# A graph layer with four gated experts on one core: a join of partitions at step 90 of the experts' loop, intermediate rows in one tensor per group, a sixth buffer in the last stage

## The chip, the cores and the metric

The kernel runs on one NeuronCore of a Trainium2 chip. The metric is the device time of one execution in microseconds (us). Before the change it is 4193.42 us, the median of 3 runs (4192.93 to 4193.94).

## What is computed

x holds 12500 nodes of 256 float32 features. Two layers are added to it, one after the other. (The helper functions of the second are written here as one line each.)

```python
x = x + gnn(layernorm(x), src, dst, edge_weight, W, b)      # 200000 edges
x = x + ffn(layernorm(x), ...)                              # 131072 edges + a loop at each node

def gnn(z, src, dst, w, W, b):
    agg = segment_sum(z[src] * w[:, None], dst)
    return agg @ W.T + b

def ffn(x, ...):                       # HEADS = 4, NUM_EXPERTS = 4, TOP_K = 2
    h = (x @ W_gat).reshape(M, 4, 4)
    e = leaky_relu((h * att_src).sum(-1)[src] + (h * att_dst).sum(-1)[dst], 0.2)
    alpha = softmax of e over the edges of one dst, for each head
    agg = segment_sum(h[src] * alpha[:, :, None], dst).reshape(M, 16) + b_gat
    scores = layernorm(agg, ln_gamma, ln_beta).reshape(M, 4, 4).mean(1)
    w = softmax(top 2 of scores)
    for ei in range(4):
        out += gate(w, ei) * (gelu(x @ W1[ei] + b1[ei]) @ W2[ei] + b2[ei])
```

So each node needs two things at the end: four rows of 256 from the four experts, which depend on the node alone, and four gates, which depend on a softmax over the edges that end at it. The edges of this second graph start and end at nodes below 8192; the other nodes have the loop only.

## The kernel before, in words

Nodes are padded to 98 tiles of 128 (`NT`) and worked on in 25 groups of 4 tiles (`GT`, `NG`; the last group has 2 tiles).

**Stage 1**, up to about 2230 us: layer norm; POOL gathers the rows of the 200000 edges (L550) and PE adds them up with one-hot products (L564). Beside it the 131072 edges of the second graph are sorted by their end.

**Stage 2, the nodes**: `node_out` makes `x2 = x + agg W^T + b` and stores it, two groups at a time, to the DRAM tensor `X2` (`x2_rows`). Then come the norm (stored turned, `y_t`), and the small features of the attention (`gat_nodes`). The profile leaves digits at the end of a word out of names: `x2_rows` shows as `x_rows`, `po5` and `po4` as `po`, `o5` as `o`.

**Stage 3, the experts**, from 2495 to 3916 us. A loop over `step` goes through 100 pairs of (group, expert), and step 100 ends the last. Step s issues on PE, half by half, `up` of pair s (products with W1, L942, then Gelu on ACT, L948, into `hh`) and `down` of pair s - 1 (products with W2, L966, into one of two PSUM buffers `po5`; then DVE adds b2, L970, into `fo`). After two experts of a group SP stores `fo` to `FO` (`expert_rows`, L974). The order of PE is written by hand in this loop (`tc.manual_schedule`): what is issued inside it on PE keeps its place. The other engines get their order from the scheduler of the framework, and each runs its own in order.

Under the experts runs the attention. The sorted edges lie on 128 partitions, 1024 columns each (`L2`), edge after edge. POOL gathers 11 columns (`PER_TURN`) of `G` per step (L809), held back so that it is no more than `LEAD` = 4 steps ahead. As soon as all columns of a `block` (128 columns; the last two are 896 to 991 and 992 to 1023) are there, DVE and ACT do a running maximum, exponentials and running sums on it (L880 to L902), in some eight parts by `yield`, one part per step, and SP stores the finished columns to `gat_run` in DRAM. The condition ahead of a block is `(step - 2) * PER_TURN >= blocks[0][1]`, so that it comes two steps behind its columns. What is left after step 100 is issued behind the loop.

**The join.** A node's edges may be split between two partitions. So the values at the end of each partition are carried on to the next: column 1024 of `G` is turned (`carried`: two PE transposes, a scan on DVE, one transpose back), with an Exp on ACT between maxima and sums. That is six PE transposes in all. Then POOL gathers one row per partition from `gat_run` (the row at which the first node of the partition ends, `row<-gat_run,fix_i`), it is corrected (`fixed`), and POOL scatters it back. All that stands behind the loop.

**Stage 4, the gates and the mix.** SP loads three small rows (L1062) and `nodes` (`gat_nodes` again, 1.2 MB, L1068). `gates(t0, n)` works on four stretches of tiles: 0 to 11, 12 to 35, 36 to 79, 80 to 97. For each tile POOL gathers one row of `gat_run` per node (`R`, L1082: the row at which the node's edges end, and for a node without edges one row at the end of the table); then follow some 50 DVE instructions with Exp, Sqrt and Exp on ACT (L1098 to L1145). `R` has two buffers, so that a third stretch waits for the first. `mixed(g)` loads `fo_in` (2 MB, L1151) and the rows of x2 (`o5`, 0.5 MB, L1154) on SP, in the pool `mix` of five buffers; per tile ACT makes a diagonal matrix (L1158), PE adds x2 and the expert of index 3 (L1160, L1161), DVE adds the other three (L1163); ACT stores to `out` (L1166). `issue_after` puts the gates of a stretch behind the last `mixed` of the stretch before.

The pools of stage 4 open after those of stage 3 are closed, and lie on the same memory.

Of the kernel before, what the change touches and what calls it, by code (L numbers as in the profile page):

```python
# [23 lines left out]
F32 = mybir.dt.float32  # L24
# [4 lines left out]
AF = mybir.ActivationFunctionType  # L29
ALU = mybir.AluOpType  # L30
AX = mybir.AxisListType
PSUM = bass.MemoryType.PSUM
# [20 lines left out]
GT = 4  # L53
# [7 lines left out]
def gnn_gat_moe(ctx, tc, x, src, dst, edge_weight, W, b, W_gat, att_src, att_dst, b_gat, ln_gamma,  # L61
# [3 lines left out]
    Z = nc.dram_tensor("z_rows", (NPAD, D), F32).ap()  # L65
    WT = nc.dram_tensor("w_turned", (D, D), F32).ap()
    STARTS = nc.dram_tensor("gat_starts", (E2 + NPAD, SEG), F32).ap()
    X2 = nc.dram_tensor("x2_rows", (NPAD, D), F32).ap()
    YT = nc.dram_tensor("y_t", (P, NT, 2, P), F32).ap()
    FO = nc.dram_tensor("expert_rows", (NPAD, C, D), F32).ap()  # L70
    NODE = nc.dram_tensor("gat_nodes", (NPAD, ROW), F32).ap()
    RUN2 = nc.dram_tensor("gat_run", (E2 + P, ROW), F32).ap()

# [12 lines left out]
    def node_rows(table, t0, n):  # L86
        return table[t0 * P:(t0 + n) * P, :].rearrange("(t p) d -> p t d", p=P)
# [569 lines left out]
    with ExitStack() as s2:  # L657
# [57 lines left out]
        def node_out(g):  # L715
            f, (t0, n, _) = flow[g], rows_of(g)
            if g % 2 == 0:
                f["x2_two"] = gp.tile([P, 2 * GT, D], F32, name="x2_two", bufs=2)
            x2_two = flow[g - g % 2]["x2_two"]
            x2 = f["x2"] = x2_two[:, g % 2 * GT:(g % 2 + 1) * GT]  # L720
            for i, m in pairs(n):
                po = ps.tile([P, 2, D], F32, name="po")
                for a in range(m):
                    for k in range(2):
                        nc.tensor.matmul(po[:, a, :], f["agt"][:, i + a, k, :], w_t[:, k, :],
                                         start=(k == 0), stop=(k == 1))
                nc.vector.tensor_add(x2[:, i:i + m, :], f["x"][:, i:i + m, :], po[:, :m, :])
            if g % 2 or g == NG - 1:
                m = g % 2 * GT + n
                nc.sync.dma_start(node_rows(X2, t0 + n - m, m), x2_two[:, :m, :])  # L730
            f["y"] = gp.tile([P, GT, D], F32, name="y")
            f["stats"] = statistics(small, x2, n)

# [50 lines left out]
    with ExitStack() as s3:  # L784
# [11 lines left out]
        low = big.tile([P, 1], F32, name="low")  # L796
        fix_i = big.tile([P, 1], I32, name="fix_i")
        spot = big.tile([P, 8], F32, name="spot")
        pre = tc.alloc_tile_pool(name="pre", bufs=1)
        far = pre.tile([P, L2], F32, name="far")  # L800
        nc.gpsimd.iota(far, pattern=[[1, L2]], base=0, channel_multiplier=0,
# [72 lines left out]
        def block(a, z):  # L874
# [21 lines left out]
            for ch in range(NS):  # L896
                if ch % 4 == 0:
# [4 lines left out]
            nc.sync.dma_start(RUN2[:E2, :].rearrange("(p l) c -> p l c", l=L2)[:, a:z, :],  # L902
                              G[:, a + 1:z + 1, :])


        blocks = [(a, min(a + 128, L2 - 32)) for a in range(0, L2 - 32, 128)] + [(L2 - 32, L2)]
        under_way = None
        with ExitStack() as s5:
# [46 lines left out]
            def down(item, half):  # L955

                g, e = item["at"]
                t0, n, _ = rows_of(g)
                if half == 0 and e % 2 == 0:
                    fos[g] = io.tile([P, GT, 2, D], F32, name="fo")  # L960
                if 2 * half < n:
                    po = pe.tile([P, 2, D], F32, name="po5", bufs=2)
                    for a in range(2):
                        i = 2 * half + a
                        for f in range(NF):
                            m = nc.tensor.matmul(po[:, a, :], item["hh"][:, f, i * P:(i + 1) * P],  # L966
                                                 w_2[:, e, f, :], start=(f == 0), stop=(f == NF - 1))
                            if half == a == f == 0:
                                after_all(m, item["there"])
                    item["last"] = nc.vector.tensor_add(  # L970
                        fos[g][:, 2 * half:2 * half + 2, e % 2, :], po,
                        b_2[:, e, None, :].to_broadcast([P, 2, D]))
                if half and e % 2:
                    nc.sync.dma_start(FO[t0 * P:(t0 + n) * P, e - 1:e + 1, :].rearrange(  # L974
                        "(t p) e d -> p t e d", p=P), fos[g][:, :n])

            yts, fos, freed = {}, {}, [[], []]
# [2 lines left out]
            with tc.manual_schedule(engines={mybir.EngineType.PE}):  # L980
                old = None
                for step in range(NG * C + 1):
                    new = dict(at=divmod(step, C)) if step < NG * C else None
                    for half in range(2):
                        if new:
                            up(new, half)
                        if old:
                            down(old, half)
                    if old:
                        turned.append(old["last"])  # L990
                        gathers(len(turned) - 1 + LEAD)
                    old = new

                    if under_way is None and blocks and (step - 2) * PER_TURN >= blocks[0][1]:
                        under_way = block(*blocks.pop(0))
                    if under_way and next(under_way, under_way) is under_way:
                        under_way = None
        for _ in under_way or ():
            pass
        for a, z in blocks:  # L1000
            for _ in block(a, z):
                pass


        tail = s3.enter_context(tc.tile_pool(name="tail", bufs=1))
        end = G[:, L2, :]
        m0 = tail.tile([P, H], F32, name="m0")
        carried(tail, low.to_broadcast([P, H]), end[:, NS:], H, ALU.add, ALU.max, LOW, m0)

        def joined(m_in, s_in, m_own, name):  # L1010

            m = tail.tile([P, H], F32, name="m_" + name)
            nc.vector.tensor_max(m, m_in, m_own)
            f = tail.tile([P, 2, H], F32, name="f_" + name)
            nc.vector.tensor_sub(f[:, 0, :], m0, m)
            nc.vector.tensor_sub(f[:, 1, :], m_own, m)
            nc.scalar.activation(f, f, AF.Exp)
            return m, f

        def by_head(v, f):  # L1020

            s = tail.tile([P, NS], F32, name="by_head", bufs=2)
            nc.vector.tensor_mul(s[:, :HC].rearrange("p (h c) -> p h c", c=C),
                                 v[:, :HC].rearrange("p (h c) -> p h c", c=C),
                                 f[:, :, None].to_broadcast([P, H, C]))
            nc.vector.tensor_mul(s[:, HC:], v[:, HC:NS], f)
            return s

        m_in = tail.tile([P, H], F32, name="m_in")
        nc.vector.tensor_scalar(m_in, m0, low, None, ALU.add)  # L1030
        _, f = joined(m_in, None, end[:, NS:], "end")
        nc.vector.tensor_scalar(f[:, 0, :], f[:, 0, :], through, None, ALU.mult)
        v = by_head(end, f[:, 1, :])
        fs = tail.tile([P, NS], F32, name="fs")
        nc.vector.tensor_copy(fs[:, :HC].rearrange("p (h c) -> p h c", c=C),
                              f[:, 0, :, None].to_broadcast([P, H, C]))
        nc.vector.tensor_copy(fs[:, HC:], f[:, 0, :])
        s0 = tail.tile([P, NS], F32, name="s0")
        carried(tail, fs, v, NS, ALU.mult, ALU.add, 0.0, s0)

        row = tail.tile([P, ROW], F32, name="row")
        nc.gpsimd.indirect_dma_start(out=row, out_offset=None, in_=RUN2,
                                     in_offset=IND(ap=fix_i, axis=0))
        fixed = tail.tile([P, ROW], F32, name="fixed")
        m, f = joined(m0, None, row[:, NS:], "row")
        s_in, s_own = by_head(s0, f[:, 0, :]), by_head(row, f[:, 1, :])
        nc.vector.tensor_add(fixed[:, :NS], s_in, s_own)
        nc.vector.tensor_copy(fixed[:, NS:], m)
        nc.gpsimd.indirect_dma_start(out=RUN2, out_offset=IND(ap=fix_i, axis=0), in_=fixed,
                                     in_offset=None)  # L1050


    with ExitStack() as s4:
        one = s4.enter_context(tc.tile_pool(name="one", bufs=1))
        some = s4.enter_context(tc.tile_pool(name="some", bufs=2))
        mix = s4.enter_context(tc.tile_pool(name="mix", bufs=5))
        turn = s4.enter_context(tc.tile_pool(name="turn", bufs=4))
        ps = s4.enter_context(tc.tile_pool(name="ps4", bufs=6, space=PSUM))

        def along_nodes(ap, name):  # L1060
            t = one.tile([P, HC], F32, name=name)
# [85 lines left out]
        def mixed(g):  # L1147

            t0, n, rows = rows_of(g)
            fo = mix.tile([P, GT, C, D], F32, name="fo_in")  # L1150
            nc.sync.dma_start(fo[:, :n], FO[t0 * P:(t0 + n) * P].rearrange(  # L1151
                "(t p) e d -> p t e d", p=P))
            xo = mix.tile([P, GT, D], F32, name="o5")
            nc.sync.dma_start(xo[:, :n, :], node_rows(X2, t0, n))  # L1154
            for i in range(n):
                g4 = gate[:, t0 + i, :]
                diag = turn.tile([P, P], F32, name="diag")
# [46 lines left out]
```

## Time and profile before

| | us |
|---|---|
| median of 3 runs | 4193.42 |
| the profiled execution | 4198.22 |
| its span | 4196.4 |
| PE busy | 3552.0 (85%) |
| POOL busy | 2906.0 (69%) |
| DVE busy | 2393.0 (57%) |
| ACT busy | 1421.4 (34%) |
| 3500 to 3916 (experts): PE busy; DMA share; GB/s | 399.99 of 416; 0.22; 59 |
| 3916 to 4196 (join and last stage): PE busy; DVE busy; DMA share; GB/s | 125.19 of 280; 193.81; 0.91; 286 |

The profile is of one execution. Its page has a row per engine with the busy share of 40 equal slices of the span, in tenths, and a row with the GB/s that the DMA engines moved. A window view gives for any stretch its length, the busy time and number of instructions of PE, PE's weight loads, DVE, ACT and POOL, the clock granted to PE (1.00 is full), the share of 16 DMA engines that were busy, and GB/s. A timeline gives start, duration, engine, line and tiles of each instruction; in brackets stands the idle time ahead and what ended it. The chain of waits goes back from the last instruction to what released each step. The largest steps of it that lie near the end are loads and stores, and the gathers of `R`:

```profile
3942.41 5.74 DMA R<-gat_run,end
...
4024.91 49.50 DMA fo_in<-expert_rows
4074.42 10.90 DMA o<-x_rows
4098.46 10.38 DMA out<-o
```

### The profile page before, as it was taken

Reading aid. Unit: us, or ns where it says so; the run is one execution under the profiler, and the core shown is the slowest. Engines: PE = TensorE matmul, PEld = TensorE weight load, DVE = VectorE, ACT = ScalarE, POOL = GpSimd, SP = SyncE. Lnnn points to the kernel's source line nnn. Section 1 sums busy time; section 2 is a strip of 40 time slices with the busy share of each in tenths; the row PEclk is TensorE's granted clock in tenths of the full one; section 3 lists DMA queues with packets and bytes.
Section 4 is the critical chain, followed back from the end, with each engine's and each line's share of the span. In section 5 each row is a group of like instructions: output and inputs, shape, how many; then the busy total and the mean of one; then the engine's idle time right before and its main releaser. Section 6 shows DMA issues by size and latency. Waiting matters only on the chain. (4 is left out here: it accounts for less than half of the span.)

```text
span 4196.4 us, 54596 instructions
## 1 busy us (share of the span) xinstructions
PE 3552.0 (85%) x18969; PEld 2610.1 (62%) x18970; DVE 2393.0 (57%) x5474; ACT 1421.4 (34%) x3289; POOL 2906.0 (69%) x2855
## 2 busy tenths in 40 slices
PE   1466899999999999999998959999989999899545
PEld 0365676767766667767677836666656666566424
DVE  7566777878787878787778950221211202212477
ACT  4322445445545444545452211221212212212122
POOL 2577777777777777777776777777777777773440
PEclk6688999999999999999999969999999999999767
DMA  7433333333333333333335652222222222221698
GB/s 234 135 93 93 102 102 100 100 100 101 100 101 100 99 101 101 100 101 100 99 102 157 191 145 60 67 72 55 64 50 75 75 55 64 65 60 62 206 226 346
DMA packets 265845, 457.42 MB, mean 109 GB/s; under 512 B 67943, under 2 KB 168705, under 8 KB 264289
## 3 DMA queue, kind: packets, MB, share of 16 engines
q0 software_dynamic: 114128, 219.11, 21.4%
q1 hardware_dynamic: 111663, 207.52, 14.0%
q10 hardware_dynamic: 39778, 27.28, 2.1%
q8 instruction: 153, 2.51, 0.2%
q14 instruction: 123, 1.01, 0.1%
HBM read 334.05 MB, written 119.66 MB: 108 GB/s over the span
## 5 line engine op out<-in xcount | busy, mean ns | idle before, releaser
L550 POOL DMA_INDIRECT gt<-z_rows,src x1563 | 1605.2, 1027 | 592.2 <-issue 410.2
L809 POOL DMA_INDIRECT G<-gat_nodes,order x1024 | 1026.5, 1002 | 339.3 <-issue 289.0
L564 PE MATMUL win<-gt,oh_w 128*128 128x256 f32 x3126 | 770.1, 398 | 200.4 <-DMA gt<-z_rows,src 149.3
L564 PEld LDWEIGHTS win<-gt,oh_w 128*128 128x128 f32 x3126 | 598.0, 198 | 317.0 <-issue 188.4
L966 PE MATMUL po<-w,hh 128*128 128x256 f32 x3136 | 724.3, 385 | 51.4 <-ACT hh L948 38.3
L966 PEld LDWEIGHTS po<-w,hh 128*128 128x128 f32 x3136 | 605.5, 193 | 220.8 <-issue 87.1
L970 DVE TENSOR_TENSOR fo<-po,b 128x512 f32<-128x512 f32 x196 | 135.3, 690 | 1016.6 <-PE po L966 1016.6
L942 PE MATMUL ph<-yt,w 128*128 128x512 f32 (+1 forms) x1600 | 707.8, 586 | 2.8 <-DMA w<-in_L_ffn_W 2.8
L556 ACT ACTIVATE oh_w<-hit_w,w 128x128 f32<-128x128 bf16 x1563 | 500.9, 390 | 448.2 <-PE win L564 226.6
L490 DVE TENSOR_SCALAR st<-along,place_l,code 128x1024 bf16<-128x1024 f16 x1024 | 550.3, 578 | 162.3 <-PE perm L498 161.7
L948 ACT ACTIVATE hh<-ph,b 128x512 f32<-128x512 f32 (+1 forms) x400 | 249.3, 676 | 1001.6 <-PE ph L942 1001.5
L498 PE MATMUL perm<-st,to_p 128*128 128x512 bf16 x2048 | 524.1, 378 | 0.0
L942 PEld LDWEIGHTS ph<-yt,w 128*128 128x128 f32 x1600 | 305.0, 191 | 292.5 <-issue 277.9
L454 PE MATMUL look<-next,oht 98*128 98x128 f32 x2044 | 393.8, 300 | 0.0
L454 PEld LDWEIGHTS look<-next,oht 98*128 98x128 f32 x2044 | 309.6, 192 | 37.5
L462 ACT ACTIVATE next<-place 98x256 f32<-98x256 f32 x511 | 196.1, 384 | 345.1 <-PE place L459 344.3
L469 DVE TENSOR_TENSOR sel<-look,oh_lo 128x512 f32<-128x512 f32 x256 | 174.9, 683 | 186.4 <-PE look L454 185.2
L498 PEld LDWEIGHTS <-to_p 128*128 128x128 bf16 x2048 | 178.5, 97 | 122.3 <-DVE st L490 0.4
L571 DVE SCALAR_TENSOR_TENSOR acc_x<-win,in,acc_x 128x256 f32 x522 | 246.9, 473 | 8.7 <-PE win L564 8.6
L450 PE MATMUL look<-oh_lo,same_hi 128*128 128x128 bf16 x1024 | 228.1, 223 | 1.2 <-ACT next L462 1.0
L442 ACT ACTIVATE same_hi<-bank 128x512 bf16<-128x512 f32 x256 | 152.8, 597 | 215.2 <-PE bank L440 215.1
L340 DVE TENSOR_TENSOR oh_hi<-twice,hi 128x784 bf16<-128x784 bf16 x256 | 143.4, 560 | 100.6 <-PE place L364 100.5
(278 smaller groups left out, 3641.8 us busy)
## 6 DMA issues: line engine op xcount, KB each, us to landing
expert_rows<-fo SPq DMA_DIRECT2D x48, 1024.0 KB, 4.2
fo_in<-expert_rows SPq DMA_DIRECT2D x24, 2048.0 KB, 16.4
gt<-z_rows,src POOLq DMA_INDIRECT x1563
G<-gat_nodes,order POOLq DMA_INDIRECT x1024
xt<-in_x SPq DMA_DIRECT2D x24, 512.0 KB, 4.8
z_rows<-xt ACTq DMA_DIRECT2D x24, 512.0 KB, 4.6
x_two<-in_x SPq DMA_DIRECT2D x12, 1024.0 KB, 6.4
x_rows<-x_two SPq DMA_DIRECT2D x12, 1024.0 KB, 10.6
```

Of the source, the lines that this page charges most:

```text
L450: first = nc.tensor.matmul(look[:, i % GT + k, :], b["m"][:, i + k, :], one(b["ol"], i + k), start=True, stop=False)
L454: nc.tensor.matmul(look[:, i % GT + k, :], b["oht"][:, i + k, :], nxt[:, k, :], start=False, stop=True)
L490: last = nc.vector.tensor_scalar(st[:, k, :], along, b["l"][:, i + k:i + k + 1], code2[:, c:c + 1], ALU.is_equal, ALU.mult)
L498: first = nc.tensor.matmul(perm[:, h, :], one(b["p"], i + k), st[:, k, h * 512:(h + 1) * 512], start=(c == 0), stop=(c == NC2 - 1), skip_g ...
L550: there = [nc.gpsimd.indirect_dma_start(out=rows[j], out_offset=None, in_=Z, in_offset=IND(ap=idx[:, c:c + 1], axis=0)) for j, c in enumer ...
L556: there += [nc.scalar.activation(hots[j], one(hit, j), AF.Copy, scale=w[:, c:c + 1]) for j, c in enumerate(chunks)]
L564: i = nc.tensor.matmul(win, h, r, start=(j == 0), stop=(j == len(rows) - 1))
L571: return nc.vector.scalar_tensor_tensor(to, win, m, to, ALU.mult, ALU.add)
L809: i = nc.gpsimd.indirect_dma_start(out=G[:, t + 1, :], out_offset=None, in_=NODE, in_offset=IND(ap=order[:, t:t + 1], axis=0))
L942: i = nc.tensor.matmul(ph[:, :n], w_1[:, e, k, f * P:(f + 1) * P], yts[g][:, :n, k, :], start=(k == 0), stop=(k == 1))
L948: i = nc.scalar.activation(item["hh"][:, f, :n * P], ph[:, :n].rearrange("p t m -> p (t m)"), AF.Gelu, bias=b_1[:, e * NF + f:e * NF + f + 1])
L966: m = nc.tensor.matmul(po[:, a, :], item["hh"][:, f, i * P:(i + 1) * P], w_2[:, e, f, :], start=(f == 0), stop=(f == NF - 1))
```

## The change

Six edits, in stages 2 to 4.

1. `X2` becomes one DRAM tensor per two groups, and `FO` one per group, instead of one each; stores and loads use the part that they need.
2. A block no longer comes two steps behind its columns. The block of columns 896 to 991 counts as there at column 990, which is step 90. When only the last two blocks are left (and none is under way), all parts that are left are issued in one step, in place of one part per step.
3. The join becomes a function, `join()`, and is called in the loop where the last block ends. Its code is that of before, but for a copy: column 1024 is copied into a tile `end` first, so that `join` reads that. The pool `tail` opens at the start of stage 3.
4. Stores of `fo` of the last three groups (22 to 24) are issued by ScalarE's queue in place of SP's.
5. The pools of stage 4 get `reuse_waits="tile"`: a tile waits for the tiles that lay on its own memory, rather than for all of a pool's.
6. `mix` has six buffers in place of five.

```diff
-    X2 = nc.dram_tensor("x2_rows", (NPAD, D), F32).ap()
+    X2 = [nc.dram_tensor(f"x2_rows{g}", (2 * GT * P, D), F32).ap() for g in range((NG + 1) // 2)]
-    FO = nc.dram_tensor("expert_rows", (NPAD, C, D), F32).ap()
+    FO = [nc.dram_tensor(f"expert_rows{g}", (GT * P, C, D), F32).ap() for g in range(NG)]
...
+        def join():
+            end = tail.tile([P, ROW], F32, name="end")
+            nc.vector.tensor_copy(end, G[:, L2, :])
...
-                    nc.sync.dma_start(FO[t0 * P:(t0 + n) * P, e - 1:e + 1, :].rearrange(
+                    queue = nc.sync if g < NG - 3 else nc.scalar
+                    queue.dma_start(FO[g][:n * P, e - 1:e + 1, :].rearrange(
...
-                    if under_way is None and blocks and (step - 2) * PER_TURN >= blocks[0][1]:
-                        under_way = block(*blocks.pop(0))
-                    if under_way and next(under_way, under_way) is under_way:
-                        under_way = None
-        for _ in under_way or ():
-            pass
-        for a, z in blocks:
-            for _ in block(a, z):
-                pass
...
+                    for _ in range(1 if len(blocks) > 2 or under_way and len(blocks) == 2 else 20):
+                        if under_way is None and blocks and step * PER_TURN >= min(
+                                blocks[0][1], (L2 - 32) // PER_TURN * PER_TURN):
+                            under_way = block(*blocks.pop(0))
+                        if under_way and next(under_way, under_way) is under_way:
+                            under_way = None
+                            if not blocks:
+                                join()
+                assert not blocks and under_way is None
...
-        mix = s4.enter_context(tc.tile_pool(name="mix", bufs=5))
+        mix = s4.enter_context(tc.tile_pool(name="mix", bufs=6, reuse_waits="tile"))
...
-            nc.sync.dma_start(fo[:, :n], FO[t0 * P:(t0 + n) * P].rearrange(
-                "(t p) e d -> p t e d", p=P))
+            nc.sync.dma_start(fo[:, :n], FO[g][:n * P].rearrange("(t p) e d -> p t e d", p=P))
-            nc.sync.dma_start(xo[:, :n, :], node_rows(X2, t0, n))
+            nc.sync.dma_start(xo[:, :n, :], node_rows(X2[g // 2], g % 2 * GT, n))
```

More of the change, by code (lines that the diff above doesn't have):

```diff
@@ L729, in node_out @@
                 m = g % 2 * GT + n
-                nc.sync.dma_start(node_rows(X2, t0 + n - m, m), x2_two[:, :m, :])
+                nc.sync.dma_start(node_rows(X2[g // 2], 0, m), x2_two[:, :m, :])
             f["y"] = gp.tile([P, GT, D], F32, name="y")
@@ L798, in gnn_gat_moe @@
         spot = big.tile([P, 8], F32, name="spot")
+        tail = s3.enter_context(tc.tile_pool(name="tail", bufs=1))
         pre = tc.alloc_tile_pool(name="pre", bufs=1)
@@ L903, in block, with joined, by_head @@
                               G[:, a + 1:z + 1, :])
+        def join():
+            end = tail.tile([P, ROW], F32, name="end")
+            nc.vector.tensor_copy(end, G[:, L2, :])
+            m0 = tail.tile([P, H], F32, name="m0")
+            carried(tail, low.to_broadcast([P, H]), end[:, NS:], H, ALU.add, ALU.max, LOW, m0)
+            def joined(m_in, s_in, m_own, name):
+                m = tail.tile([P, H], F32, name="m_" + name)
+                nc.vector.tensor_max(m, m_in, m_own)
+                f = tail.tile([P, 2, H], F32, name="f_" + name)
+                nc.vector.tensor_sub(f[:, 0, :], m0, m)
+                nc.vector.tensor_sub(f[:, 1, :], m_own, m)
+                nc.scalar.activation(f, f, AF.Exp)
+                return m, f
+            def by_head(v, f):
+                s = tail.tile([P, NS], F32, name="by_head", bufs=2)
+                nc.vector.tensor_mul(s[:, :HC].rearrange("p (h c) -> p h c", c=C),
+                                     v[:, :HC].rearrange("p (h c) -> p h c", c=C),
+                                     f[:, :, None].to_broadcast([P, H, C]))
+                nc.vector.tensor_mul(s[:, HC:], v[:, HC:NS], f)
+                return s
+            m_in = tail.tile([P, H], F32, name="m_in")
+            nc.vector.tensor_scalar(m_in, m0, low, None, ALU.add)
+            _, f = joined(m_in, None, end[:, NS:], "end")
+            nc.vector.tensor_scalar(f[:, 0, :], f[:, 0, :], through, None, ALU.mult)
+            v = by_head(end, f[:, 1, :])
+            fs = tail.tile([P, NS], F32, name="fs")
+            nc.vector.tensor_copy(fs[:, :HC].rearrange("p (h c) -> p h c", c=C),
+                                  f[:, 0, :, None].to_broadcast([P, H, C]))
+            nc.vector.tensor_copy(fs[:, HC:], f[:, 0, :])
+            s0 = tail.tile([P, NS], F32, name="s0")
+            carried(tail, fs, v, NS, ALU.mult, ALU.add, 0.0, s0)
+            row = tail.tile([P, ROW], F32, name="row")
+            nc.gpsimd.indirect_dma_start(out=row, out_offset=None, in_=RUN2,
+                                         in_offset=IND(ap=fix_i, axis=0))
+            fixed = tail.tile([P, ROW], F32, name="fixed")
+            m, f = joined(m0, None, row[:, NS:], "row")
+            s_in, s_own = by_head(s0, f[:, 0, :]), by_head(row, f[:, 1, :])
+            nc.vector.tensor_add(fixed[:, :NS], s_in, s_own)
+            nc.vector.tensor_copy(fixed[:, NS:], m)
+            nc.gpsimd.indirect_dma_start(out=RUN2, out_offset=IND(ap=fix_i, axis=0), in_=fixed,
+                                         in_offset=None)
@@ L992, in gnn_gat_moe @@
                     old = new
-                    if under_way is None and blocks and (step - 2) * PER_TURN >= blocks[0][1]:
-                        under_way = block(*blocks.pop(0))
-                    if under_way and next(under_way, under_way) is under_way:
-                        under_way = None
-        for _ in under_way or ():
-            pass
-        for a, z in blocks:
-            for _ in block(a, z):
-                pass
-        tail = s3.enter_context(tc.tile_pool(name="tail", bufs=1))
@@ L1006, in gnn_gat_moe @@
[L1006 to L1050, printed above, removed]
@@ L1053, in gnn_gat_moe @@
-    with ExitStack() as s4:
-        one = s4.enter_context(tc.tile_pool(name="one", bufs=1))
-        some = s4.enter_context(tc.tile_pool(name="some", bufs=2))
-        mix = s4.enter_context(tc.tile_pool(name="mix", bufs=5))
-        turn = s4.enter_context(tc.tile_pool(name="turn", bufs=4))
-        ps = s4.enter_context(tc.tile_pool(name="ps4", bufs=6, space=PSUM))
+                    for _ in range(1 if len(blocks) > 2 or under_way and len(blocks) == 2 else 20):
[6 more added lines that the diff above has]
+                                join()
@@ new lines, in gnn_gat_moe @@
+                assert not blocks and under_way is None
+    with ExitStack() as s4:
+        one = s4.enter_context(tc.tile_pool(name="one", bufs=1, reuse_waits="tile"))
+        some = s4.enter_context(tc.tile_pool(name="some", bufs=2, reuse_waits="tile"))
+        mix = s4.enter_context(tc.tile_pool(name="mix", bufs=6, reuse_waits="tile"))
+        turn = s4.enter_context(tc.tile_pool(name="turn", bufs=4, reuse_waits="tile"))
+        ps = s4.enter_context(tc.tile_pool(name="ps4", bufs=6, space=PSUM, reuse_waits="tile"))
```

## The prediction

> **What bounds the kernel now.** I read the busy slices first, then a table of windows over the end of the run, then the engines' timelines and DMA queues there. The change touches only what runs after about 3800 us.
>
> ```profile
> PE   1466899999999999999998959999989999899545
> POOL 2577777777777777777776777777777777773440
> GB/s 234 135 93 93 102 102 100 100 100 101 100 101 100 99 101 101 100 101 100 99 102 157 191 145 60 67 72 55 64 50 75 75 55 64 65 60 62 206 226 346
> ```
>
> The experts (slices 25 to 37) keep PE at nine tenths with 50 to 75 GB/s: PE-bound. In the last three slices PE falls to half and the bytes rise. The windows split that end (after the engines: granted clock, DMA share, GB/s):
>
> ```profile
> 3900.00:3916.30 16.30, 15.41 (x71) 12.90 (x69) 1.41 (x3) 2.95 (x8) 0.00 (x0) 1.00 0.09 34
> 3916.30:3939.00 22.70, 1.08 (x4) 0.42 (x4) 5.12 (x30) 1.70 (x3) 10.59 (x11) 0.59 0.59 80
> 3939.00:4000.00 61.00, 20.09 (x60) 13.74 (x60) 45.22 (x161) 11.41 (x24) 45.77 (x48) 0.58 1.02 381
> 4000.00:4008.50 8.50, 7.98 (x25) 6.61 (x26) 6.68 (x17) 4.49 (x12) 6.37 (x8) 0.66 0.16 17
> 4008.50:4070.00 61.50, 21.08 (x69) 14.59 (x67) 38.07 (x89) 8.21 (x17) 32.82 (x35) 0.64 0.99 161
> 4070.00:4152.50 82.50, 53.70 (x168) 40.91 (x168) 61.81 (x162) 17.69 (x45) 0.00 (x0) 0.75 1.04 406
> 4152.50:4196.40 43.90, 21.03 (x72) 15.57 (x72) 36.88 (x118) 10.36 (x24) 0.00 (x0) 0.73 0.68 263
> ```
>
> PE's last expert product ends at 3916.2. Then 23 us pass in the join and the small loads. From 3939 the DMA engines are full (share 1), but for 8.5 us without a free buffer (0.16) and for 61.5 us at 161 GB/s instead of 406. Group 19 is mixed at 4152.5; after it come the last gates and 4.5 groups on DVE, 43.9 us. So the last stage is DMA-bound until 4152.5.
>
> The slow stretch is the POOL gathers of R (queue q0 over 3940 to 3990, then 4020 to 4070):
>
> ```profile
> q0 software_dynamic: 1204, 0.46, 3.9%
> q0 software_dynamic: 957, 0.37, 61.1%
> ```
>
> Fewer bytes, sixteen times the engines' time. Edges end below node 8192 = tile 64, and the kernel gives a node without edges the last row of the runs; so the gathers of tiles 64 to 97 read one row 128 times. By POOL's timeline tile 36 issues at 3973.99, and 28 issues of 1.25 us later is 4009, where the stretch begins. It loses 61.5 x (406 - 161) / 406 = 37 us for 34 gathers, 1.09 each.
>
> **Part by part.** All times are on the profiled execution (4198.2 us, span 4196.4); the median of the runs is 4193.4, so I subtract the change of the span from the median.
>
> *Up to step 90.* PE, DVE, ACT and POOL have the same order in both built kernels: the condition two steps earlier moves nothing, since the blocks already stood where their gathers land. 0.
>
> *The join in PE's hand-written order.* Its six transposes now stand between `down` of step 89 and `up` of step 91. PE cannot pass them.
>
> ```profile
> 3807.53 3.60 PE L942 MATMUL ph<-yt,w 128*128 128x512 f32 x8
> 3821.61 0.29 DVE L880 TENSOR_TENSOR G<-G,starts 128x128 f32<-128x128 f32 x1 [13.19 <-DMA G<-gat_nodes,order]
> 3825.30 4.22 DVE L899 TENSOR_TENSOR_SCAN G<-starts,G 128x32 f32<-128x32 f32 x20
> 3826.89 5.41 PE L966 MATMUL po<-w,hh 128*128 128x256 f32 x16 [1.98 <-ACT hh L948]
> 3912.51 3.72 PE L966 MATMUL po<-w,hh 128*128 128x256 f32 x16 [0.82 <-ACT hh L948]
> ```
>
> PE would start step 91 at 3807.5, but the last gather lands at 3821.6. The last block then runs to 3829.4, less one `fo` add of 0.6 that PE no longer feeds in between: 3828.9. The join from its first row copy (3917.07) to its last transpose (3923.56) took 6.5; 1.28 goes because Exp is still loaded, and the copy of the last column with its transpose adds 0.4: 3834.5. PE idles 27 us. The fourth line shows what idling costs afterwards: 5.41 for 16 products instead of 3.62, so +1.8 at half clock.
>
> *The wait that takes its place.* The rest of the join and the first gates now stand among the experts' work on ACT and DVE, both in order. The last store of the runs issues at 3829 and lands about 3832.6 (3.6, the 512 KB load of yt; an estimate). The row gather and the load of `nodes` both wait for it. The gather alone took 3.1 us (3917.70 to 3920.8), but
>
> ```profile
> 3930.33 10.57 DMA R<-gat_run,end
> ```
>
> is a gather beside `nodes`, which takes 12.4 to land. Between 3.1 and 12.4 I take the latter, since the nearest row is such a gather: row at 3845.0, `fixed` 1.4 later, 3.5 to the first R (3924.32 to 3927.80), 12 gathers of 1.25, and 2 to land: 3866.7.
>
> Queued behind this R on DVE is the add of `down` step 90, second half; it frees the second of two `po5` buffers, which `down` step 91, second half, needs. PE gets there at 3834.5 + 1.8 + 7 half steps of 3.45 = 3860.5, waits until 3868.0, and is slow by 1.8 again: done at 3873.3, before at 3839.0, +34. On ACT the gates' Exp and root, with table loads of 1.28 between Exp, root and Gelu, stand ahead of `hh` of step 92; root follows Exp by 5.7 (3949.67 to 3955.33), so `hh` is 2.9 late once more. **The experts end at 3916.2 + 37 = 3953.**
>
> *Stores on ACT.* Six issues of 0.38 (the row of `out`); ACT idles 5.6 of every 6.9 us there. 0, and 2.3 without that cover.
>
> *Split tensors, waits by tile.* No instruction is added, and `fo_in` of group 0 comes early (2.1 MB). But the next in SP's order, `o5` of group 0, waits for the last expert product: its memory is that of the experts' weights. So groups 1 to 5 load only from 3953. The layout may change the rate: full windows give 381 to 409 GB/s, up to 10 us more; I take 406, that of the longest one.
>
> *The last stage.* Before, 61 x 381 + 61.5 x 161 + 82.5 x 406 GB/s = 66.7 MB moved until group 19 was mixed. Now 2.1 MB are early, and 80 of 98 R gathers (0.9 MB) run under the experts, 16 of the slow ones among them: 63.7 MB / 406 = 157 us. The 18 left, which wait for the second gates, cost 18 x 1.09 = 19.6. The 8.5 us without a buffer go: a sixth one holds 6.5 us of loads more, and the slow gathers now fall there. What is late next is DVE, not bound: 80 tiles of 1.18 and two gates of 22 and 30 are 146 us. Group 19: 3953 + 0.3 + 157 + 19.6 = 4130. The tail's gates and 4.5 groups stay: 43.9.
>
> Span 4174, 22.4 less: **4171 us**.
>
> **Rivals.**
> 1. *DMA queues alternate* (0.20). The row gather does not wait for `nodes`: row at 3835.7, R at 3857.4, no hold of the buffer, only ACT's: experts end at 3945.5, time 4163. Against it: 10.57 beside 3.1. The Trainium skill, DMA: Bandwidth & Descriptors (Queues, rings and completion order), says each engine goes round its queues packet by packet, which would be this case; the 10.57 us row does not decide it, since several gathers were under way.
> 2. *The prefetch works* (0.08): were `o5` free earlier, five groups (13.6 MB, 33 us) would lie under the experts: 4138. For it: six buffers, a DMA share of 0.09 there. Against it: SP's order and that wait.
> 3. *The slow stretch is not the gathers* (0.12), but these addresses or stores: it stays whole, +17: 4188, within 0.2%. For it: stores to `out` overlap it; against it: the 61% of q0.
> 4. *Slower: PE stays at half clock* (0.06). After the 27 us stall 109 us of expert products remain, each us at half clock loses half. Nothing is left from 45 us of it, 0.2% slower from 62; if all, +99: 4270. Against it: the 5.41 row is followed by 3.60. The Trainium skill, TensorE: Matmul & The Clock Gate (Seeing it yourself), reports a clock stuck at a quarter for over 50 us, which here would lose 37: 4208; no window of this trace is under 0.50.
>
> **How the numbers follow.** The forecast has 0.50; 0.04 is left for a longer hold of ACT or DVE: with R at the stretch's pace (26 in 50 us, 1.92 each), a slow landing and a slow scatter R lands at 3892, +25: 4196. The range 4148 to 4190 holds forecast and rivals 1 and 3, with 20 us either way for landings and rate. Cases 2 and 4 are left out. A measurement can tell about 0.2% (8.4 us) here. Faster: forecast and rivals 1 and 2, 0.80 with a part of 3 taken and a part of the forecast's late side given; same 0.12; slower 0.08.
>
> **What would show it.** An idle PE of about 27 us behind step 89, ended by DVE; a second hold of 7 us or none (rival 1); PE's last expert product near 3953; one early `fo_in`, the others after it; one slow stretch of about 35 us, in the first third of the last stage; DMA share 1 otherwise; 44 us from group 19 to the end. Wrong would be: loads under the experts, a clock below 1 for long, or the experts ending past 3978.

## The result, and the profile after

The changed kernel takes 4168.94 us (median of 5 runs, 4165.6 to 4177.73), the one before 4193.92 in the same comparison (5 runs): a ratio of **0.9943, interval 0.9929 to 0.9957**, 25 us less. The forecast was 4171, faster. The profiled execution took 4168.61, with a span of 4166.9, where 4174 was worked out.

The page's busy slices of the changed kernel, the rows that were shown of before (the last two slices now carry 353 and 342 GB/s):

```profile
PE   1476899999999999999998959999998999997846
...
POOL 2477777777777777777776777777777777775610
...
GB/s 231 137 93 92 100 102 102 101 102 99 100 101 100 101 99 101 102 100 101 101 100 144 192 151 72 70 50 75 65 61 60 75 61 64 61 60 92 77 353 342
```

The end of the run by windows (length; busy time of PE, PE's weight loads, DVE, ACT, POOL; granted clock; DMA share; GB/s):

```profile
3805.70:3832.00 26.30, 1.73 (x7) 0.55 (x5) 11.10 (x49) 2.00 (x4) 9.99 (x11) 0.60 0.24 67
3832.00:3947.50 115.50, 109.23 (x401) 77.89 (x400) 24.39 (x88) 29.37 (x48) 76.78 (x81) 0.96 0.41 71
3947.50:3980.00 32.50, 17.75 (x57) 13.62 (x56) 20.60 (x53) 7.51 (x16) 0.00 (x0) 0.84 1.00 376
3980.00:4015.00 35.00, 17.36 (x56) 12.88 (x56) 30.83 (x93) 9.49 (x23) 17.27 (x18) 0.71 1.01 242
4015.00:4062.00 47.00, 15.35 (x44) 11.15 (x44) 36.03 (x92) 5.71 (x12) 0.00 (x0) 0.65 1.05 408
4062.00:4070.00 8.00, 7.90 (x26) 6.60 (x27) 6.60 (x17) 4.21 (x13) 0.00 (x0) 0.70 0.91 349
4070.00:4123.30 53.30, 38.63 (x140) 27.05 (x138) 45.86 (x116) 12.77 (x32) 0.00 (x0) 0.90 1.03 382
4123.30:4166.90 43.60, 22.70 (x72) 15.95 (x72) 36.51 (x118) 10.36 (x24) 0.00 (x0) 0.71 0.76 292
```

First line: PE idles for 26 us at the join. Second: the rest of the experts, with 77 us of POOL's gathers under them. Then the loads: full, one slow stretch of 35 us with 18 gathers (242 GB/s), full again. Group 19 is mixed at 4123.3, 43.6 us ahead of the end.

PE's timeline (start, duration, line; in brackets the idle time ahead):

```profile
3802.26 3.62 PE L1017 MATMUL po<-w,hh 128*128 128x256 f32 x16
...
3827.12 0.37 PE L826 MATMUL pt<-ident,end 128*4 128x128 f32 x1 [21.13 <-DVE end L910]
...
3832.01 6.74 PE L993 MATMUL ph<-yt,w 128*128 128x512 f32 x8
...
3862.38 5.23 PE L1017 MATMUL po<-w,hh 128*128 128x256 f32 x16 [2.97 <-DVE fo L1021]
...
3873.64 3.72 PE L1017 MATMUL po<-w,hh 128*128 128x256 f32 x16 [2.37 <-ACT hh L999]
...
3943.80 3.72 PE L1017 MATMUL po<-w,hh 128*128 128x256 f32 x16 [0.93 <-ACT hh L999]
```

The join holds PE from 3806.0 to 3832.0. R holds it twice more, by DVE for 2.97 us and by ACT for 2.37. The wait of 0.93 us ahead of the last product has nothing to do with R: it was there before, with 0.82. The last product of the experts ends at 3947.5, 31 us later than before.

To compare executions that reach the end of the gathers of `G` a few us apart, the table counts from the issue of the last of these gathers (3818.4 before, 3816.5 after), to the experts' last product, the start of the last gates (group 19 mixed) and the end of the span. Ratios are to the kernel before on the same chip; e1 to e4, e5 to e8 and e9 to e12 ran on three chips, so kernels of different groups are compared by their ratios.

| kernel | ratio (interval) | experts' end | last gates | end |
|---|---|---|---|---|
| before | 1 | 97.8 | 334.5 | 378.0 |
| after | 0.9943 (0.9929 to 0.9957) | 131.0 | 306.8 | 350.4 |
| e1 join behind | 0.9978 (0.9969 to 0.9987) | 97.4 | 317.4 | 361.0 |
| e2 join only | 0.9959 (0.9945 to 0.9973) | 123.8 | 317.4 | 361.2 |
| e3 five buffers | 0.9962 (0.9949 to 0.9976) | 130.1 | 314.0 | 357.5 |
| e4 own rows | 0.9917 (0.9904 to 0.9931) | 129.5 | 297.6 | 341.2 |
| e9 memory | 0.9914 (0.9901 to 0.9928) | 133.5 | 297.2 | 341.0 |
| e10 own rows, join at 92 | 0.9853 (0.9838 to 0.9868) | 107.9 | 273.9 | 317.5 |
| e11 all three | 0.9856 (0.9841 to 0.9871) | 110.0 | 268.6 | 312.1 |
| e12 and second gates | 0.9813 (0.9800 to 0.9826) | 111.7 | 258.5 | 302.2 |

From before to after: the experts 33 us later, the last stage from there to group 19 shorter by 61 (236.7 to 175.8), the tail as it was.

### The profile page after: what moved, and what is told of

The parts are those of the page before. It is cut to its first block, busy times and chain, and to the rows that moved or that the text cites. A ratio compares the mean times of both kernels' runs of the same rounds, so it can differ in the third digit from the quotient of the medians.

```text
span 4166.9 us, 54584 instructions
## 1 busy us (share of the span) xinstructions
PE 3554.4 (85%) x18969; PEld 2611.2 (63%) x18970; DVE 2395.5 (57%) x5475; ACT 1425.0 (34%) x3293; POOL 2901.1 (70%) x2855
## 5 line engine op out<-in xcount | busy, mean ns | idle before, releaser
L1017 PE MATMUL po<-w,hh 128*128 128x256 f32 x3136 | 724.1, 385 | 53.1 <-ACT hh L999 37.5
L1017 PEld LDWEIGHTS po<-w,hh 128*128 128x128 f32 x3136 | 606.0, 194 | 222.1 <-issue 86.5
```

## The experiments

**e1: all but the join in the loop.** Blocks and join stand where they stood; the rest is the changed kernel.

```diff
+                    if under_way is None and blocks and (step - 2) * PER_TURN >= blocks[0][1]:
...
+        for a, z in blocks:
+            for _ in block(a, z):
+                pass
+        join()
```

> The changed kernel, but blocks and join stand where they stood before: two steps behind their columns, the join behind the loop, outside PE's hand-written order. Account A (the prediction's: what counts is when the loads of the last stage start, the bytes at 406 GB/s, and 1.09 us for each slow gather that runs beside them): the experts end at 3916 as before, since nothing holds PE; the loads wait for the join alone and no longer for nodes, so they start near 3923 in place of 3939, with 2.6 MB (6.5 us) already there, and the sixth buffer fills the 8.5 us without one; all 34 slow gathers stay beside the loads. 3923 + (66.7 - 2.6) MB / 406 + 37 = 4118, tail 43.9: a span near 4162, a time of 4160 to 4172, so about that of the changed kernel. Rival B (the gain is that join and gates lie under the experts): all of it is lost, 4185 to 4194.

4180.98 (11 runs): between the two accounts, so A's sum lacked something. Windows of e1:

```profile
3916.00:3944.00 28.00, 3.55 (x8) 1.85 (x6) 6.60 (x27) 2.24 (x5) 20.80 (x22) 0.50 0.98 375
3944.00:3965.00 21.00, 12.29 (x43) 10.03 (x44) 18.16 (x65) 5.64 (x14) 15.82 (x18) 0.67 0.52 175
3965.00:4005.00 40.00, 18.71 (x66) 12.56 (x66) 35.75 (x110) 11.63 (x27) 30.25 (x33) 0.74 0.84 289
4005.00:4052.00 47.00, 12.44 (x39) 7.95 (x38) 34.68 (x86) 4.61 (x8) 28.48 (x28) 0.65 1.00 144
```

The loads start at 3916, sooner than expected, and fill six buffers by 3944; then they run dry (shares 0.52 and 0.84), because the first gates are there only at 3951.6 and the second at 3987.8: the first gathers start behind the join at 3916.8, one per 1.25 us, and the second gates are issued behind the mixing of group 2. All 34 slow gathers lie beside the loads, too (144 GB/s in the last window), where the changed kernel has 18; how the loss divides between the late gates and these 16 gathers, no run separates. So what the join in the loop pays for is this chain, join, gathers and gates, and not the loads' start. The join in the loop holds the experts for 33 us and is still worth 11 us at the end by the traces (361.0 against 350.4), 15 by the ratios.

**e2: the join at step 90 alone.** x2 and the experts' rows in one tensor each, stores on SP, five buffers, no `reuse_waits`. (It is also dropped from three pools of the stages ahead, `turning`, `hot` and `gathered`, which have it in the kernels before and after. The last gather of `G` issues at 3816.71 here and at 3816.54 in the changed kernel, so nothing of that is seen up to there.)

> Only the blocks and the join at step 90; one tensor each for x2 and the experts' rows, stores on SP, five buffers, the pools' waits as before. Account A: the experts end near 3947 as in the changed kernel (join in PE's order, hold by DVE and ACT), 80 gathers lie under them; fo_in of group 0 is not early (+5.2 us) and a buffer is missing (0 to +8.5): 4174 to 4183. Rival B would have the same; a rival D, in which it is the waits of the new pools and the early load that carry the gain, gives 4190 or more, since PE's stall of 31 us is then not paid back.

4174.95, as A had it; rival D falls. By the ratios the join in the loop alone takes 17 us off (e2), all the rest alone 9 (e1), and both together 24. Edits 1, 4 and 5 were not tried one by one. The trace shows something not expected: the experts end 7 us sooner than in the changed kernel. POOL's timeline of the changed kernel, and then of e2:

```profile
3830.29 0.94 POOL L946 DMA_INDIRECT row<-gat_run,fix_i  x1 [12.80 <-DMA bg<-in_L_ffn_b_gat]
3841.98 1.00 POOL L953 DMA_INDIRECT gat_run<-fixed,fix_i  x1 [10.75 <-DVE fixed L951]
```

```profile
3830.25 0.95 POOL L946 DMA_INDIRECT row<-gat_run,fix_i  x1 [12.60 <-DMA gat_run<-G]
3834.16 1.00 POOL L953 DMA_INDIRECT gat_run<-fixed,fix_i  x1 [2.96 <-DVE fixed L951]
```

In the changed kernel `nodes` (1.2 MB) was issued at 3829.50, just ahead of `row`, which landed at 3840.3; in e2 `nodes` came at 3837.99, and `row` landed at 3832.5: 10.1 us against 2.3. That is the hold which the prediction chose between 3.1 and 12.4.

**e3: five buffers.**

```diff
-        mix = s4.enter_context(tc.tile_pool(name="mix", bufs=6, reuse_waits="tile"))
+        mix = s4.enter_context(tc.tile_pool(name="mix", bufs=5, reuse_waits="tile"))
```

> The changed kernel with five buffers in the last stage. Account A: with one group less ahead (6.5 us of loads), the loads run dry once or twice while the gates hold DVE (30 us for 44 tiles, five buffers hold 32 us): 0 to +8.5 us, 4172 taken. Rival: the buffer does nothing because DVE, not DMA, sets the pace of the last stage by now: 4169 within 0.1%.

4175.36. The trace shows 7.1 us more (357.5 against 350.4); by the times, 0.9962 and 0.9943 have overlapping intervals, so the buffer's worth is seen in the one execution only.

**e4: own rows for nodes without edges.**

```diff
+            nc.vector.tensor_scalar_add(begin, node, -float(E2))
+            nc.vector.tensor_sub(last, last, begin)
+            nc.vector.tensor_mul(last, last, has)
+            nc.vector.tensor_add(last, last, begin)
             by_node(last, end2)
```

> The changed kernel, where a node without edges gathers the row of its own number in place of the table's last row (its value is masked either way); so the gathers of tiles 64 to 97 read 128 different rows each. Account A: the slow stretch of the last stage goes, 18 gathers x 1.09 = 19.6 us less: 4149; the share of the gathers' queue in the DMA engines over the gathers' time falls from about a half to a few per cent. Rival C (the stretch is slow for another reason, the addresses of these groups or the stores to out): it stays, 4169.

4156.22: rival C falls. The gathers' queue in the windows that hold them (packets, MB, share of the DMA engines), 3980 to 4020 of the changed kernel, and 3980 to 4003 of e4:

```profile
q0 software_dynamic: 576, 0.22, 31.3%
```

```profile
q0 software_dynamic: 545, 0.21, 3.3%
```

A gather is 32 packets, so the first window has all 18 gathers and the second 17 of them. All 16 DMA engines' time per gather falls from 0.70 us (0.313 x 40 / 18) to 0.04 (0.033 x 23 / 17), about what the fast gathers of before take (3.9% of 50 us for 1204 packets: 0.05). The window moves 407 GB/s in place of 262. But the end comes 9 us sooner by the traces and 11 by the ratios, not 14 to 20, since something is late next:

```profile
4003.00:4036.00 33.00, 15.66 (x52) 9.17 (x52) 31.67 (x76) 6.16 (x12) 0.00 (x0) 0.79 1.05 406
4036.00:4054.20 18.20, 6.68 (x19) 5.40 (x20) 15.45 (x46) 4.31 (x12) 0.00 (x0) 0.54 0.80 316
4054.20:4075.00 20.80, 20.24 (x79) 13.44 (x77) 20.80 (x54) 7.75 (x20) 0.00 (x0) 1.00 0.96 320
```

DVE is busy for 31.67 of 33, 15.45 of 18.2 and 20.8 of 20.8 us: while it does the third gates (4020.2 to 4047.0) no buffer comes free, the loads pause (0.80), and then it catches up.

**e5 to e8** (the changed kernel, and the edits of e9, e10 and e11 below) ran on a chip where every kernel took 18% longer, so that only their stages can be read.

> The changed kernel once more, on the chip of the next three, as the base for them: 0.9943 of the kernel before, as measured, give or take 0.0014.

> The changed kernel with the memory of the last stage laid out so that it does not wait for the experts: the rows of x2 (o5) in a pool of their own at the bottom, fo_in in two pools of three, the lower of which lies on the dead G. Account A (SP's next load waits for o5's memory, that of the experts' weights): the loads of three fo_in and six o5, 9.4 MB in place of 2.1, go out near 3846 under the experts; 7.3 MB / 406 = 18 us less behind them. The price: these 23 us of full DMA lie on the 12 gathers of the first gates, whose R then lands late and holds DVE, ACT and PE longer, 0 to 10 us. In all 8 to 18 us less than the changed kernel: 0.990 to 0.992 of before. Rival (DVE and the gates set the pace of the last stage): the loads move and the time does not, 0.994.

> The kernel of e4 (own rows for nodes without edges) with the join called two steps later, at step 92; the blocks stay where they are. Account A (PE stands idle for 21 us behind step 89 only because the join's transposes are fixed there ahead of step 91's work): two steps of 13.8 lie ahead of them now, the last column is there when PE arrives, and about 5 us of the join's own chain are left; the row and R are no later, since the gathers wait for the stores and not for PE. The experts end 20 us sooner, near 3923, and so does all behind: 0.987 of before (4136). Rival (the gates' gathers, which end at 3945 in any case, or DVE set the pace): 0.9917 as in e4.

> All three: join at step 92, own rows, and the memory of e6. Account A: the two gains of e7 and e6 add up, less what the hold by R takes: 30 to 38 us under e4, 0.983 to 0.985 of before (4118 to 4128). If DVE is the bound by then (98 tiles of 1.18 and gates of 19, 28 and 18 us are 181 us, from 3926 on: 4107 at the soonest), it is 0.984 as the floor. Rival: as e7.

Measured: before 4963.56, e5 4961.86 (0.9996, interval 0.9968 to 1.0025), e6 4955.67 (0.9979, 0.9948 to 1.0010), e7 4935.92 (0.9951, 0.9930 to 0.9971), e8 4934.99 (0.9939, 0.9907 to 0.9971). All four miss the time that was expected. The interval of e5 does not reach 0.9943: on this chip the gain of the change was not seen. The base's own runs spread there from 4929 to 5000, and nothing under 0.3% can be told. From the loads' release to the end their traces have 221.9, 210.3, 213.3 and 205.5 us, in e5 about the 219 of the changed kernel.

**e9: memory that does not wait for the experts** (as e6).

```diff
+        rows5 = s4.enter_context(tc.tile_pool(name="rows5", bufs=6, reuse_waits="tile"))
...
-        mix = s4.enter_context(tc.tile_pool(name="mix", bufs=6, reuse_waits="tile"))
+        mix = s4.enter_context(tc.tile_pool(name="mix", bufs=3, reuse_waits="tile"))
+        mix2 = s4.enter_context(tc.tile_pool(name="mix2", bufs=3, reuse_waits="tile"))
...
-            fo = mix.tile([P, GT, C, D], F32, name="fo_in")
+            fo = (mix2 if g // 3 % 2 else mix).tile([P, GT, C, D], F32, name="fo_in")
...
-            xo = mix.tile([P, GT, D], F32, name="o5")
+            xo = rows5.tile([P, GT, D], F32, name="o5")
```

> The kernel of e6 again, since the chip of e5 to e8 ran every kernel 18% slower (before: 4963.56), with engines waiting for their own instructions everywhere. There the last stage, from the experts' last product to the end, was 11.6 us shorter than in e5 (210.3 and 221.9 us). Account A as for e6: 8 to 18 us under the changed kernel, 0.990 to 0.992 of before. Rival: 0.994.

4159.78, 12 us under the changed kernel by the ratios and 9 by the traces: A, in the lower half. SP's waits in the changed kernel, from 3945 to the end (waited for, us, times, longest), name the block: one wait of 101 us.

```profile
SPq L1159 <- PE po L1017: 101.0, 1, 101.0
```

In e9 three `fo_in` and six `o5` go out from 3852 on, under the experts. The price came too: the first R lands at 3870.1 and PE is held 5.68 and 2.60 us, 3 more than in the changed kernel.

**e10: e4 with the join at step 92** (as e7; the blocks stay at 90).

```diff
-                            if not blocks:
-                                join()
+                    if step == 92:
+                        join()
```

> The kernel of e7 again. Account A: PE's idle time behind step 89 goes (21 us), 5 us of the join's own chain stay, the experts end near 3923: 0.987 of before (4136 where before is 4191). Rival: 0.9917 as in e4.

4132.92, as A had it and 3 us better; the rival falls. PE's timeline of e10:

```profile
3833.80 0.27 PE L830 MATMUL pt<-ident,end 128*4 128x128 f32 x1
3835.47 0.23 PE L842 MATMUL pt<-ident,carried 4*128 4x4 f32 x1 [1.39 <-DVE carried L840]
3838.42 0.39 PE L830 MATMUL pt<-ident,fs 128*20 128x128 f32 x1 [2.72 <-DVE fs L945]
...
3840.06 5.21 PE L997 MATMUL ph<-yt,w 128*128 128x512 f32 x8
```

The transposes find their data there, and 6 us are left of the 26. So 20 of the 26 us were bought by the place in PE's order alone.

**e11: e10 with the memory of e9.**

> The kernel of e8 again. Account A: 0.983 to 0.985 of before (4118 to 4128); by e8's last stage (205.5 us against 213.3 in e7) the memory is worth 8 us where own rows are there already, which gives 4128. Rival: as in e10.

4134.41: not under e10 (0.9856 and 0.9853). A's time fails here. Windows of e11:

```profile
3960.00:3980.00 20.00, 10.74 (x39) 8.97 (x40) 17.20 (x56) 6.37 (x18) 13.46 (x15) 0.65 0.73 255
3980.00:4000.00 20.00, 15.78 (x55) 8.78 (x53) 19.96 (x53) 3.29 (x9) 0.00 (x0) 1.00 1.00 349
...
4020.00:4040.00 20.00, 13.63 (x48) 10.92 (x48) 17.42 (x53) 7.24 (x19) 0.00 (x0) 0.70 0.65 237
4040.00:4060.00 20.00, 16.96 (x63) 10.84 (x64) 20.00 (x52) 6.29 (x16) 0.00 (x0) 1.00 1.03 360
```

The loads that come sooner run dry sooner (0.73, 0.65): behind each gates DVE has 20 of 20 us of mixing to catch up. Yet the traces do not say that the memory is worth nothing. From the experts' end to group 19, e11 takes 158.6 us where e10 takes 166.0, and by the table it is 5 us ahead of e10 at the end; but its last gather of `G` issues at 3821.31, 8.3 us after that of e10 (3813.03), although the two kernels differ only in the memory of stage 4. Whether that late start belongs to e11 or to this one execution, no kept trace shows; so it stays open whether the two gains add up in the last stage.

**e12: the second gates under the experts.**

```diff
+                        if step == 97:
+                            second = old["last"]
...
-            with tc.issue_after(last.ins) if last else ExitStack():
+            hold = second if t0 == 12 else last
+            with tc.issue_after(hold.ins) if hold else ExitStack():
```

> The kernel of e11, and the second gates (24 tiles, 19 us of DVE) no longer wait for group 2 but for the experts' pair 96: DVE, idle four fifths of the time there, does them under the last experts. In e8 DVE was busy 182 of 205 us in the last stage and the loads ran dry three times behind gates. If DVE is what is late next, as account A has it, 10 to 19 us go, less 3 to 6 us that PE waits for ACT's table loads and DVE: 4110 to 4121 where before is 4191 (0.981 to 0.983). Rival (DMA alone sets the pace): nothing, or 3 to 6 us more than e11.

4115.91, 18 us under e11 and **0.9813 of before** (0.9800 to 0.9826): the best version, some 54 us under the changed kernel by the ratios. The rival (DMA alone) falls: moving the second gates under the experts, and no load, makes the last stage shorter. By the traces the stretch from the experts' end to group 19 goes from 158.6 to 146.8 us, while DVE's busy time in it falls from 138.20 to 124.95; the end, counted from the last gather of `G`, comes 9.9 us sooner (312.1 to 302.2). The times have 18; in the two traced executions 5.6 us of the difference lie ahead of that last gather (3821.31 and 3815.69), where neither edit acts. Against e10, the two readings agree: 17 us by the times, 15 by the traces. So DVE's work was late in e11, and was worth 10 us at the end by the traces; that all of the 18 are due to it is not shown. In e12 the DMA engines are full over that stretch (share 1.00; 0.95 in e11). The expectation misread e8: DVE was busy there for 174.6 of 205.5 us, not 182.

## Why the prediction was right, point by point

- **PE's order.** 27 us of idling were forecast behind step 89, ended by DVE; 26.0 came. Right, and e10 shows it to be the order and no need of the data. The products after it were slow by 3.1 us (6.74 against 3.60 for 8), where +1.8 was taken.
- **The hold behind R.** Forecast: R at 3866.7, PE held 7.5 us by DVE and 2.9 by ACT. Measured: 3861.3, 2.97 and 2.37. The mechanism is right, the DVE term too large by 4.5. R came 5.4 us sooner: 2.3 because the gathers of `G` ended sooner in this execution, which moved PE as well, and 2.3 because `row` landed in 10.1 us where 12.4 was taken. PE, held longer by its slow products, came 1.1 sooner only. (The terms as written add up to 3866.9.) Rival 1's second mark, no hold of the buffer, is not seen after, but in e2, where `row` went ahead of `nodes`, only 0.85 us of ACT is left. The rule of the Trainium skill, DMA: Bandwidth & Descriptors (Queues, rings and completion order), that an engine alternates between queues by packet, would let a small gather through; here it came 8 us later for having 1.2 MB issued 0.8 us ahead of it on another queue (10.1 against 2.3). Why, no run here shows.
- **The experts' end.** 3953 forecast, 3947.5 measured: these 5.5 us are most of the 7.1 by which the span (4174) was too long.
- **Early loads.** One `fo_in` at 3846.06, all others from 3947.5 on, after SP's wait of 101 us for the experts' last product. Right. Rival 2's condition was made true in part by e9 (9.4 MB early, where the rival had 13.6), which gave 9 to 12 us where 4138 stood for 33.
- **The last stage.** From the experts' end to group 19: 176.9 forecast (0.3 + 157 + 19.6), 175.8 measured. (The bytes of before add up to 66.6 MB, not 66.7; the 157 stays.) The parts by the windows: 63.0 MB (the sum of length times GB/s) at 406 are 155.2, and 157 was taken; the slow stretch loses 35 x (406 - 242) / 406 = 14.1, and 19.6 was taken, 0.78 each in place of 1.09; the rest, 6.5 us, is the start and the windows behind 4062, and 0.3 was taken. So the total came out right by luck, by two errors of some 6 us that cancel: the slow gathers were dearer in the forecast than in the chip, and the loads' pauses behind the third gates were not in it.
- **No buffer.** "a sixth one holds 6.5 us of loads more": 7.1 by e3's trace, and not clear of the noise by the times.
- **The tail.** 43.9 forecast, 43.6 measured.
- **Rival 3** (the stretch is not the gathers) falls with e4. **Rival 4** (PE at half clock to the end) falls: 0.96 over the 115 us behind the join. The stuck clock of the Trainium skill, TensorE: Matmul & The Clock Gate (Seeing it yourself), did not occur in any window shown here; the lowest granted clock in them is 0.50.
- What the prediction did not see: it wrote of the last stage that what is late next is "DVE, not bound", with 146 us. With 175.8 us that held for the stage as a whole, but not for each part of it: the loads' pauses above come from DVE. e1 shows how near it was: without the join in the loop the gates are late and 11 of the 28 us at the end are lost, in part perhaps by the slow gathers. e4 and e12 show that it ends with the next step.

## What to carry to other kernels

An instruction put into a hand-written order is a wait for all that stands behind it: ask when its data is there, and put it where the engine arrives no sooner (two steps here, 20 us). Where a stage is full on one resource, count the next one as well, with its own bursts: loads that come sooner are worth little once the buffers wait for DVE (5 us by the trace of e11, nothing by its times). And a gather with an index that stands for "none" should not send all rows to one address.

## What the hardware showed that was not expected

- A gather of 128 rows of 96 bytes cost all 16 DMA engines 0.70 us (in the changed kernel; 1.09 was worked out from before) when all read one row, and 0.04 when they read 128 different rows (e4, where they are neighbours).
- A small gather on POOL's queue took 10.1 us with a 1.2 MB load issued 0.8 us ahead of it on SP's, 2.3 without (e2). In e9, where `row` went 0.7 us ahead of `nodes`, it took 3.0, and the scatter behind it held the first R for 8.1 us instead.
- On one chip the same kernels took 4900 to 5000 us. The time is lost ahead of the last stage, which takes 221.9 us in e5 and 219.4 in the changed kernel's first execution. Far more of the engines' idle time is put down to their own issue there, beside waits for other engines. In the changed kernel's first execution the idle time of PE ahead of the W2 products (L1017) is 53.1 us, all of it put down to ACT and DVE; in e5 it is 213.2, of which 161.4 are "issue". The waits of e5 (us in total, times, longest):

```profile
ACT hh L999 <- issue: 236.2, 31, 51.2
...
DVE fo L1021 <- issue: 170.1, 29, 10.1
...
PE po L1017 <- issue: 161.4, 109, 7.5
```

Why that chip issues so slowly is open.
